# An LSTM layer with a residual: the last four, not eight, steps from plain products in two half banks each, a new column order, and a new order at the head

## The chip, the core and the metric

The kernel runs on one core of a Trainium2 chip. TensorE multiplies into PSUM (eight banks, 128 partitions of 512 fp32 each), ScalarE and VectorE do the element-wise work, GpSimd adds the residual, and SyncE (SP) issues the DMAs. The metric is the device time of one execution in microseconds (us), the median of three runs. A profiled execution of the same program gives the page and the trace that are quoted; it has its own time and, within that, its span from the first to the last recorded instruction.

## What is computed

```
x: (32, 512, 512)   h0: (32, 512)   Wx, Wh: (512, 2048)   b: (2048)
xW = x @ Wx + b                       # per step t: (32, 2048), gates i f o g
c  = 0;  h = h0
for t in 0..511:
    a = xW[:, t] + h @ Wh
    c = sigmoid(a_f) * c + sigmoid(a_i) * tanh(a_g)
    h = sigmoid(a_o) * tanh(c)
    out[:, t] = x[:, t] + h
```

All of it is in fp32. The steps are a chain: step t + 1 needs the h of step t.

## The kernel before

**Layout.** A step's pre-activations a fill one PSUM bank: partition j * 32 + b for the j-th block of 128 units and batch row b, and along the free axis four gates (G) of 128 units. A product with 512 columns is four matmul calls, one for each j, on four column groups of TensorE; each fp32 call shows as two MATMUL instructions in the trace. The banks are three accumulators pa, one pb, one pp, and the gate banks ge (even steps) and go[0], go[1] (odd steps), chosen by gates_of (L88).

**The input product.** Four consecutive steps are a quad. For quads FIRST = 2 to LAST - 1 = 125 (steps 8 to 503), x Wx of the four steps is made by a fast matrix product in two levels (Strassen's scheme in Winograd's form): 7 outer products r = 1 to 7, each of 7 inner products s = 1 to 7, that is 49 products of 128 columns in place of the 64 that plain products have. Operands are sums of blocks of x (early_sums L115, late_sums L132) and differences of blocks of Wx (outer_weight L196, inner_weight L200, scheduled by weights and make_weights). Results are collected by adds, copies and seeds in evacuate (L385), and end in the gate banks before h Wh is added there. Each r runs in its own windows (BEGIN), and input_part (L420) issues those of window k.

**Plain products.** Steps 0 to 7 and 504 to 511 have x Wx from direct (L345): for each of four pairs (k, gg), two blocks e and four j, 256 columns each. At the end these go to the banks in last_banks as the fast products release them; which pair goes into which window is set by the loop over todo (L551), by the room left beside the fast products. The bias enters by a copy into the bank ahead (set_bias) or an add behind (add_bias). reload (L209) brings back part of the raw Wx, which w_5 had overwritten.

**The order.** All instructions are put out in program order per engine (manual_schedule), with no reordering by a planner. The loop over windows k = 8 to 522 does, for step t = k - 11: h_part(t) (L448: h Wh, 16 calls of 512 columns), then evacuate, bias, sums and weights for VectorE and ScalarE, then input_part and direct as TensorE's filler, then cell(t) (L460). h_part(t + 1) waits for the transposed h of cell(t), so the filler is what TensorE does while the cell runs. In cell, sigmoid (i, f), tanh (g) and sigmoid (o) are three ScalarE instructions over all 128 units of a partition; products, sum, tanh of c, h and the transpose go in two halves of 64 units, so that h_part(t + 1) can begin with the first half (ht[:, 0:2]).

**The head.** SP issues, in this order, the bias row, chunk 0 of x (eight steps), raw Wx (0,0), chunk 1, raw (0,1), (1,0), (1,1), h0 and Wh in quarters. TensorE clears banks (clear, first_bias), then runs first_direct (L534), plain products of steps 2, 0, 1 and 3 while the raw weights arrive, and step 4's into pp.

**The end.** After step 511, x is added to the transposed halves of h in the tile last (L491), and one DMA stores it (L492).

Of the kernel before, what the change touches and what calls it, by code (L numbers as in the profile page):

```python
# [11 lines left out]
P = 128  # L12
B = 32
# [6 lines left out]
FIRST = 2  # L20
LAST = T // 4 - 2

LEAD = 11
BEGIN = {1: 0, 5: 1, 6: 3, 7: 6, 2: 7, 3: 7, 4: 9}
WINDOWS = T + LEAD


@with_exitstack
def kernel(
# [7 lines left out]
    out: bass.AP,  # L37
):


# [45 lines left out]

    last_banks = [pa[1], pa[0], pp, pb, pa[2], go[0], ge, go[1]]

    def gates_of(t):
        if t >= 4 * LAST:  # L90
            return last_banks[t - 4 * LAST]
        return ge if t % 2 == 0 else go[(t % 4) // 2]
# [85 lines left out]
    def load_raw(k, gg):  # L178
# [3 lines left out]
        )  # L182

    bias_row = w_sb[7][0:1, 0:NJ].rearrange("p s j u -> p s (j u)")
    nc.sync.dma_start(out=bias_row, in_=bias.rearrange("j g u -> j (g u)").unsqueeze(0))
    load_chunk(0)
    load_raw(0, 0)
    load_chunk(1)
    load_raw(0, 1)
    load_raw(1, 0)  # L190
    load_raw(1, 1)
    nc.sync.dma_start(out=h_init.rearrange("p q b -> p (q b)"), in_=h0)
    for k in range(NJ):
# [37 lines left out]

    def clear(bank):

        for j in range(NJ):
            nc.tensor.matmul(
                bank[j * B : (j + 1) * B],
                c_init[:, 0:B],
                c_init.unsqueeze(1).to_broadcast([P, 4, P]),
                start=True,
                stop=True,  # L240
            )

    def first_bias(bank):

        for j in range(NJ):
            nc.tensor.matmul(bank[j * B : (j + 1) * B], ones, bias_row[:, j], start=True, stop=True)
# [97 lines left out]

    def direct(t, pairs, bank=None):  # L345

        c, tt = divmod(t, TC)
        bank = gates_of(t) if bank is None else bank
        fresh = not written(bank)
        for k, gg in pairs:  # L350
            for e in range(2):
                for j in range(NJ):
                    nc.tensor.matmul(  # L353
                        bank[j * B : (j + 1) * B, 2 * gg : 2 * gg + 2],
                        xcs[c][:, tt, 2 * k + e],
                        raw_blocks(k, gg, e, t >= 4 * LAST)[:, :, j],
                        start=fresh and (k, gg, e) == (0, 0, 0),
                        stop=True,
                        skip_group_check=True,
                    )  # L360
# [86 lines left out]
    state = {"c": c_init, "ht": h_init}  # L447

    def h_part(t):
        g = gates_of(t)  # L450
        for k in range(NJ):
            for j in range(NJ):
                nc.tensor.matmul(  # L453
                    g[j * B : (j + 1) * B],
                    state["ht"][:, k, :],
                    wh_sb[:, k, j, :],
                    start=False,
                    stop=True,
                    skip_group_check=True,
                )  # L460

    def cell(t):
        n, tt = divmod(t, TC)
        g = gates_of(t)
        s = work.tile([P, G, P], F32, name=f"s_{t}", tag="s")
        nc.scalar.activation(s[:, 0:2, :], g[:, 0:2, :], AF.Sigmoid)  # L466
        nc.scalar.activation(s[:, 3, :], g[:, 3, :], AF.Tanh)
        nc.scalar.activation(s[:, 2, :], g[:, 2, :], AF.Sigmoid)
        fc = work.tile([P, P], F32, name=f"fc_{t}", tag="fc")
# [3 lines left out]
        ht = work.tile([P, NJ, B], F32, name=f"ht_{t}", tag="ht", bufs=3)  # L473
        halves = [slice(0, P // 2), slice(P // 2, P)]
        nc.vector.tensor_mul(fc, s[:, 1, :], state["c"])  # L475
        for u in halves:
            nc.vector.tensor_mul(ig[:, u], s[:, 0, u], s[:, 3, u])  # L477
        for u in halves:
            nc.vector.tensor_add(c[:, u], fc[:, u], ig[:, u])  # L479
        for u in halves:  # L480
            nc.scalar.activation(tc_t[:, u], c[:, u], AF.Tanh)  # L481
        for u in halves:
            nc.vector.tensor_mul(h[:, u], s[:, 2, u], tc_t[:, u])  # L483
        for i, u in enumerate(halves):
            nc.vector.transpose(ht[:, 2 * i : 2 * i + 2].rearrange("p q b -> p (q b)"), h[:, u])  # L485
        state["c"], state["ht"] = c, ht
        if t == T - 1:
            last = opool.tile([P, 2, NJ, B], F32, name="last", tag="oc")
            for i in range(2):
                q = slice(2 * i, 2 * i + 2)  # L490
                nc.vector.tensor_add(last[:, 0, q], xcs[n][:, tt, q], ht[:, q])  # L491
            nc.sync.dma_start(out=out[n][:, tt * P :], in_=last[:, 0].rearrange("p q b -> p (q b)"))  # L492
            return
        if tt % 2 == 0:
# [11 lines left out]
        0: [(5, 6)],  # L506
        1: [(1, 4), (5, 7), 6, (6, 5)],
        2: [(5, 4), (6, 6)],
        3: [(6, 7)],
# [19 lines left out]
    bias_at = {12: (2,), 13: (5,), 14: (4,), 15: (7,), 16: (6,)}  # L529
    direct_at = {k: [(t, ALL) for t in bias_at[k] if t not in (2, 4)] for k in bias_at}  # L530
    direct_at[11], direct_at[12] = [(3, ALL[2:3])], [(3, ALL[3:4])]

    def first_direct(k):

        pairs = {8: ALL[0:2], 9: ALL[2:3], 10: ALL[3:4]}.get(k, ())
        for pair in pairs:
            direct(2, (pair,), gates_of(3))
            if k == 10:
                park(2, gates_of(3), "u3")
                set_bias(3)  # L540
            for t in (0, 1):
                direct(t, (pair,))
        if k == 10:
            direct(3, ALL[0:2])

    end = 4 * LAST
    free_at = (504, 509, 510, 510, 512, 513, 514, 515)
    todo = [(end + i, (pair,)) for i in range(8) for pair in ALL]
    bias_after = {}
    for k in range(504, WINDOWS):  # L550
        bias_at[k] = tuple(end + i for i in range(8) if free_at[i] == k and written(gates_of(end + i)))  # L551
        count = sum(
            n
            for r in BEGIN
            for stage, n in enumerate((2, 1, 1, 2 if r == 2 else 3, 1 if r == 2 else 0))
            if quad_at(r, k, stage) is not None
        )
        room = (12 - count) // 4 if k < 513 else 2 + k % 2
        direct_at[k] = []
        while todo and free_at[todo[0][0] - end] <= k and room > 0:  # L560
            t = todo[0][0]
            direct_at[k].append(todo.pop(0))
            room -= 1
            if not written(gates_of(t)):
                bias_after[t] = k + 1
        assert not todo or todo[0][0] > k - LEAD + 1
    assert not todo

    with tc.manual_schedule():
        warm = work.tile([P, G, P], F32, name="warm", tag="s")  # L570
        nc.scalar.activation(warm[:, 0], c_init, AF.Sigmoid)
        nc.vector.memset(xr1, 0.0)
        for bank in (go[1], ge):
            clear(bank)
        first_bias(pp)
        clear(go[0])
        nc.vector.tensor_copy(go[1], pp)
        nc.scalar.copy(bias_sb, pp)
        for t in (0, 1):
            set_bias(t)  # L580
        make((1, 5))
        make((1, 6))
        start_sums()
        first = early_sums(nc.vector, 1)
        for op in first[:6]:
            op()
        make((1, 7))
        make(5)
        for op in first[6:]:
            op()  # L590
        make((5, 5))
        early, late = {}, {}
        for k in range(4 * FIRST, WINDOWS):
# [4 lines left out]
            if k == 4 * LAST + 1:  # L598
                reload()
            if t >= 0:  # L600
                h_part(t)
            evacuate(k)
            for i in bias_at.get(k, ()):
                set_bias(i)
            for i in bias_after:
                if bias_after[i] == k:
                    add_bias(i)
            for first, sums_of, made, cut in ((-1, early_sums, early, 5), (3, late_sums, late, 3)):
                c, rest = divmod(k - first, TC)
                if (2 if sums_of is early_sums else 1) <= c < NCHUNK - 1 and rest in (0, 2):  # L610
                    if rest == 0:
                        made[c] = sums_of(nc.vector, c)
                    for op in made[c][:cut] if rest == 0 else made.pop(c)[cut:]:
                        op()
            make_weights(k)
            if t < 0:
                first_direct(k)
            input_part(k)
            if k == 10:
# [11 lines left out]
def _laid_out(name, a):  # L631
# [7 lines left out]
    elif name == "L0_cond_Wx":  # L639

        a = a.reshape(NJ, 2, 2, B, 2, 2, NJ, P).transpose(1, 4, 0, 3, 2, 5, 6, 7).reshape(4, P, 4 * NJ * P)
    elif name == "L0_cond_Wh":
        a = a.reshape(NJ, NJ, B, G, NJ, P).transpose(0, 2, 1, 4, 3, 5).reshape(P, NJ, NJ, G * P)
    else:
        a = a.reshape(G, NJ, P).transpose(1, 0, 2)
    return _np.ascontiguousarray(a)
# [22 lines left out]
```

## Time and profile before

| | us |
|---|---|
| median of 3 runs | 3161.65 |
| lowest, highest run | 3161.55, 3162.08 |
| the profiled execution | 3161.6 |
| its span | 3159.8 |
| h Wh (L453), sum of its groups, busy | 1852.3 |
| VectorE, ScalarE, GpSimd busy | 2233.7, 1275.6, 237.1 |
| DMA, mean rate over the span | 27 GB/s |

The granted TensorE clock is 9 in each of the page's 40 slices (90% of full speed or more), and 1.0 as the mean of the run. In rows of the trace, the first number is the start in the span, the second the busy time, then engine, line, operation, output and input tile, shapes and count; a bracket gives the idle time ahead of it and what released it. Matmul rows overlap: one ends later than the next one starts, so distances of starts tell the pace.

### The profile page before, as it was taken

The page shows a single profiled execution, that of the slowest core. Times are in us where ns is not written, and L with a number is a line of the kernel's source. Part 1 is how long each engine was busy: PE and PEld are TensorE (multiplying, and loading weights), DVE is VectorE, ACT ScalarE, POOL GpSimd, SP SyncE. Part 2 cuts the span into 40 slices and gives each one's busy share as a digit, 9 for nine tenths or more (in the row PEclk, how much of TensorE's full clock was granted, in tenths as well). Part 3 has the DMA queues.
Part 4 walks back from the last instruction along what each step waited for, and adds up shares of the span by engine and source line. Part 5 has one row for each costly group of instructions (what it writes and reads, how often), then busy time and mean ns, then how long its engine had stood idle before and what let it go on. Part 6 is the DMA issues. An engine that isn't in the chain of part 4 may idle for free.

```text
span 3159.8 us, 149296 instructions
## 1 busy us (share of the span) xinstructions
PE 3148.7 (100%) x66048; PEld 1897.1 (60%) x66048; DVE 2233.7 (71%) x9239; ACT 1275.6 (40%) x4191; POOL 237.1 (8%) x515
## 2 busy tenths in 40 slices
PE   9999999999999999999999999999999999999999
PEld 5666666666666666666666666666666666666653
DVE  7777777777777777777777777777777777777763
ACT  2444444444444444444444434444444444443432
POOL 0000000000000000000000000000000000000000
PEclk9999999999999999999999999999999999999999
DMA  3000000000000000000000000000000000000010
GB/s 134 28 26 21 26 21 27 26 21 26 28 20 28 20 28 26 21 26 21 26 26 21 26 28 20 28 20 28 26 21 26 23 25 28 20 26 28 20 34 13
DMA packets 48460, 86.19 MB, mean 27 GB/s; under 512 B 5313, under 2 KB 38337, under 8 KB 46785
## 3 DMA queue, kind: packets, MB, share of 16 engines
q1 hardware_dynamic: 47810, 76.64, 7.3%
q8 instruction: 516, 8.45, 1.1%
q14 instruction: 134, 1.10, 0.1%
HBM read 43.07 MB, written 33.55 MB: 24 GB/s over the span
## 4 chain that ended last, share of the span: by engine, by line
PE 99%; DVE 1%; DMA 0%; ACT 0%; issue 0%; SPq 0%; DVEq 0%; ACTq 0%
PE ge L453 28%; PE go L453 27%; PE pa L325 18%; PE pp L325 10%; PE pb L325 6%; PE ge L325 5%; PE go L325 3%; PE go L353 1%; PE pa L453 0%; PE ge L353 0%; PE pa L353 0%; DMA w<-in_L_cond_Wx_dram 0%; PE pp L353 0%; PE pp L453 0%; PE pb L453 0%; ACT s L466 0%
## 5 line engine op out<-in xcount | busy, mean ns | idle before, releaser
L453 PE MATMUL go<-wh_sb,ht 128*32 128x512 f32 x8128 | 918.7, 592 | 0.1
L453 PE MATMUL ge<-wh_sb,ht 128*32 128x512 f32 x8064 | 911.5, 592 | 1.4 <-DVE ht L485 1.2
L475 DVE TENSOR_TENSOR fc<-s,c 128x128 f32<-128x128 f32 x511 | 149.6, 293 | 566.9 <-ACT s L466 566.9
L453 PEld LDWEIGHTS go<-wh_sb,ht 128*32 128x32 f32 x8128 | 256.7, 110 | 458.3 <-issue 454.5
L453 PEld LDWEIGHTS ge<-wh_sb,ht 128*32 128x32 f32 x8064 | 256.8, 110 | 456.3 <-issue 415.6
L496 POOL TENSOR_TENSOR oc<-xc,ht 128x128 f32<-128x128 f32 x511 | 236.9, 464 | 2913.9 <-DVE ht L485 1457.9
L466 ACT ACTIVATE s<-ge 128x256 f32<-128x256 f32 x253 | 97.1, 384 | 828.8 <-PE ge L453 828.8
L325 PE MATMUL pa<-w,n 128*32 128x128 f32 x5952 | 299.2, 273 | 0.0
L481 ACT ACTIVATE ig<-c 128x64 f32<-128x64 f32 x1024 | 205.9, 248 | 222.1 <-DVE c L479 222.1
L466 ACT ACTIVATE s<-go 128x256 f32<-128x256 f32 x254 | 97.5, 384 | 442.8 <-PE go L453 442.8
L483 DVE TENSOR_TENSOR fc<-s,ig 128x64 f32<-128x64 f32 x1024 | 190.2, 225 | 96.4 <-ACT ig L481 96.4
L325 PEld LDWEIGHTS pa<-w,n 128*32 128x32 f32 x5952 | 181.1, 110 | 76.7 <-issue 39.7
L325 PEld LDWEIGHTS pa<-w,na 128*32 128x32 f32 x3968 | 124.3, 110 | 148.5 <-issue 110.5
L265 ACT COPY u<-pp 128x512 f32<-128x512 f32 x248 | 145.2, 585 | 141.9 <-PE pp L325 141.9
L325 PE MATMUL pa<-w,na 128*32 128x128 f32 x3968 | 200.0, 273 | 0.0
L325 PE MATMUL pp<-w,sa 128*32 128x128 f32 x3968 | 199.4, 273 | 0.0
L325 PE MATMUL pa<-w,nb 128*32 128x128 f32 x3968 | 199.4, 273 | 0.0
L485 DVE STREAM_TRANSPOSE ht<-fc 128x64 f32<-128x64 f32 x1024 | 190.5, 224 | 1.7 <-DVE fc L483 1.3
L477 DVE TENSOR_TENSOR ig<-s 128x64 f32<-128x64 f32 x1024 | 181.1, 218 | 0.0
L479 DVE TENSOR_TENSOR c<-fc,ig 128x64 f32<-128x64 f32 x1024 | 181.0, 218 | 0.0
L395 DVE TENSOR_TENSOR p<-u,p 128x512 f32<-128x512 f32 x124 | 86.0, 694 | 114.5 <-ACT u L265 114.5
L325 PEld LDWEIGHTS pa<-w,nb 128*32 128x32 f32 x3968 | 121.4, 110 | 74.1 <-issue 37.6
(139 smaller groups left out, 5289.2 us busy)
## 6 DMA issues: line engine op xcount, KB each, us to landing
xc<-in_x_dram SPq DMA_DIRECT2D x64, 512.0 KB, 3.9
out_dram<-oc SPq DMA_DIRECT2D x255, 128.0 KB, 1.7
w<-in_L_cond_Wx_dram SPq DMA_DIRECT2D x4, 1024.0 KB, 9.4
wh_sb<-in_L_cond_Wh_dram SPq DMA_DIRECT2D x4, 1024.0 KB, 17.9
w<-in_L_cond_Wx_dram SPq DMA_DIRECT2D x2, 512.0 KB, 6.3
h_init<-in_cond_dram SPq DMA_DIRECT2D x1, 64.0 KB, 13.5
out_dram<-oc SPq DMA_DIRECT2D x1, 64.0 KB, 1.6
out_dram<-last SPq DMA_DIRECT2D x1, 64.0 KB, 1.6
```

The costliest lines, as they stand in the source:

```text
L265: nc.scalar.copy(u, pp)
L325: nc.tensor.matmul(dst[j * B : (j + 1) * B], operand(r, s, quad), w_sb[r][:, place(r, s), j], start=start, stop=True, skip_group_check=True,)
L395: nc.vector.tensor_add(U["p5", q], U[4, q], U["p5", q])
L453: nc.tensor.matmul(g[j * B : (j + 1) * B], state["ht"][:, k, :], wh_sb[:, k, j, :], start=False, stop=True, skip_group_check=True,)
L466: nc.scalar.activation(s[:, 0:2, :], g[:, 0:2, :], AF.Sigmoid)
L475: nc.vector.tensor_mul(fc, s[:, 1, :], state["c"])
L477: nc.vector.tensor_mul(ig[:, u], s[:, 0, u], s[:, 3, u])
L479: nc.vector.tensor_add(c[:, u], fc[:, u], ig[:, u])
L481: nc.scalar.activation(tc_t[:, u], c[:, u], AF.Tanh)
L483: nc.vector.tensor_mul(h[:, u], s[:, 2, u], tc_t[:, u])
L485: nc.vector.transpose(ht[:, 2 * i : 2 * i + 2].rearrange("p q b -> p (q b)"), h[:, u])
L496: nc.gpsimd.tensor_add(state["oc"][:, tt % 2], xcs[n][:, tt], ht)
```

## The change

It does the following.

- LAST goes from 126 to 127: steps 504 to 507 become quad 126 of the fast product, and steps 508 to 511 alone are plain.
- Each of these four has two banks (last_banks is now four pairs), one for each half of the units: half_of(t, h). h_part issues h Wh for them by halves, in the order A01, B01, A23, B23 (the number is the block of h), and for step 511 A0123, B0123. cell handles half A in full, then half B.
- The columns of Wx, Wh and the bias are in the order half, gate, unit (host layout _laid_out), so that a half's four gates are together; in every cell, a gate is then two runs of 64 in the bank and in s.
- In step 511, x is added to h before any transpose (x_last is transposed in the window of step 498), each half is stored by a DMA of its own, and the host undoes the other layout.
- At the head, the bias row goes through ScalarE's DMA queue, chunk 0 is loaded in two halves (the second behind the raw weights), first_direct takes steps 1, 0, 2 and 3 with three banks cleared and the bias spread into ge, adds the bias of step 1 afterwards, and does all four steps' first two pairs together. Two pairs of step 5 move one window ahead. The weight differences of r = 6 move one window back.
- The last plain products stand in a table by window (last_at).

```diff
-LAST = T // 4 - 2
+LAST = T // 4 - 1
...
-    last_banks = [pa[1], pa[0], pp, pb, pa[2], go[0], ge, go[1]]
+    last_banks = [(pa[1], pa[0]), (pp, pb), (pa[2], go[0]), (ge, go[1])]
+
+    def half_of(t, h):
+
+        return last_banks[t - 4 * LAST][h][:, 0:2]
...
+    def load_steps(i):
+
+        if 0 not in xcs:
+            xcs[0] = xpool.tile([P, TC, NJ, B], F32, name="xc_0", tag="xc")
+        nc.sync.dma_start(
+            out=xcs[0][:, 4 * i : 4 * i + 4].rearrange("p t q b -> p (t q b)"),
+            in_=x[0][:, 4 * i * P : 4 * (i + 1) * P],
+        )
...
-    nc.sync.dma_start(out=bias_row, in_=bias.rearrange("j g u -> j (g u)").unsqueeze(0))
-    load_chunk(0)
+    nc.scalar.dma_start(out=bias_row, in_=bias.rearrange("j g u -> j (g u)").unsqueeze(0))
+    load_steps(0)
     load_raw(0, 0)
     load_chunk(1)
     load_raw(0, 1)
     load_raw(1, 0)
     load_raw(1, 1)
+    load_steps(1)
...
     def h_part(t):
-        g = gates_of(t)
-        for k in range(NJ):
+
+        if t < 4 * LAST:
+            order = [(gates_of(t).rearrange("p n u -> p (n u)"), slice(0, G * P), k) for k in range(NJ)]
+        else:
+            halves = [(half_of(t, i).rearrange("p n u -> p (n u)"), slice(i * G * H, (i + 1) * G * H)) for i in range(2)]
+            if t < T - 1:
+                order = [(*z, k) for kk in (0, 2) for z in halves for k in (kk, kk + 1)]
+            else:
+                order = [(*z, k) for z in halves for k in range(NJ)]
+        for g, u, k in order:
...
+    def x_last():
+
+        state["x"] = work.tile([P, P], F32, name="x_last")
+        nc.vector.transpose(state["x"], xcs[NCHUNK - 1][:, TC - 1].rearrange("p q b -> p (q b)"))
...
+        for part in ([(0, 1)] if t < 4 * LAST else [(0,), (1,)]):
+            g = by_gate(gates_of(t) if t < 4 * LAST else half_of(t, part[0]))
...
+            nc.scalar.activation(s[:, n2, 0:2], g[:, :, 0:2], AF.Sigmoid)
+            nc.scalar.activation(s[:, n2, 3], g[:, :, 3], AF.Tanh)
+            nc.scalar.activation(s[:, n2, 2], g[:, :, 2], AF.Sigmoid)
+            nc.vector.tensor_mul(both(fc), s[:, n2, 1], both(state["c"]))
...
+            if t == T - 1:
+                nc.vector.tensor_add(tc_t[:, units], h[:, units], state["x"][:, units])
+                nc.sync.dma_start(out=out[n][:, tt * P + units.start : tt * P + units.stop], in_=tc_t[:, units])
+                continue
...
-        1: [(1, 4), (5, 7), 6, (6, 5)],
-        2: [(5, 4), (6, 6)],
+        1: [(1, 4), (5, 7)],
+        2: [6, (6, 5), (5, 4), (6, 6)],
...
+        13: [(5, ALL[0:2])],
+        14: [(5, ALL[2:4])],
...
+        banks = {1: go[0], 0: ge, 2: go[1], 3: pp}
+        if k == 8:
+            for pair in ALL[0:2]:
+                for t in banks:
+                    direct(t, (pair,), banks[t], t == 1)
+        elif k == 9:
+            for t in (2, 0, 1):
+                direct(t, ALL[2:3], banks[t])
+        elif k == 10:
+            for t in (2, 0, 1):
+                direct(t, ALL[3:4], banks[t])
+            park(2, go[1], "u3")
+            nc.scalar.copy(go[1], pp)
+            nc.scalar.copy(pp, bias_sb)
+            add_bias(1)
...
+    free_at = ((508, 513), (514, 514), (516, 517), (518, 519))
+    last_at = {
+        509: [(0, 0, 0)],
+        511: [(0, 0, 1)],
+        513: [(0, 1, 0)],
+        514: [(0, 1, 1)],
+        515: [(1, 0, 0), (1, 0, 1)],
+        516: [(1, 1, 0), (1, 1, 1)],
+        517: [(2, 0, 0), (2, 0, 1)],
+        518: [(2, 1, 0), (2, 1, 1)],
+        519: [(3, 0, 0), (3, 0, 1)],
+        520: [(3, 1, 0)],
+        521: [(3, 1, 1)],
+    }
...
             if k == 4 * LAST + 1:
                 reload()
+                x_last()
...
+            for i, h in bias_before.get(k, ()):
+                nc.scalar.copy(half_of(i, h), bias_sb[:, 2 * h : 2 * h + 2])
+            for i, h in bias_after.get(k, ()):
+                nc.vector.tensor_add(half_of(i, h), half_of(i, h), bias_sb[:, 2 * h : 2 * h + 2])
```

## The prediction

> **What bounds the kernel now.** I read the page first: engine shares, then the chain of waits.
>
> ```profile
> PE 3148.7 (100%) x66048; PEld 1897.1 (60%) x66048; DVE 2233.7 (71%) x9239; ACT 1275.6 (40%) x4191; POOL 237.1 (8%) x515
> PE 99%; DVE 1%; DMA 0%; ACT 0%; issue 0%; SPq 0%; DVEq 0%; ACTq 0%
> ```
>
> TensorE is the bound almost everywhere, so the first question is how many columns it streams. A busy PE hides short stalls, though, because a matmul's row lasts longer than its issue slot. So I next took the PE timeline and read starts, not durations:
>
> ```profile
> 1003.99 3.62 PE L453 MATMUL go<-wh_sb,ht 128*32 128x512 f32 x32
> 1007.43 0.40 PE L325 MATMUL pa<-w,n 128*32 128x128 f32 x8
> 1007.64 0.40 PE L325 MATMUL pa<-w,na 128*32 128x128 f32 x8
> ...
> 1010.26 3.62 PE L453 MATMUL ge<-wh_sb,ht 128*32 128x512 f32 x32
> ...
> 1016.54 3.62 PE L453 MATMUL go<-wh_sb,ht 128*32 128x512 f32 x32
> ...
> 1022.59 3.62 PE L453 MATMUL ge<-wh_sb,ht 128*32 128x512 f32 x32
> ```
>
> h Wh takes 3.43 us from its start to the next row; an input product of 128 columns (8 instructions; I call it a **unit**) takes 0.2185. A steady step is 3.43 + 0.2185 f with f = 13, 13, 12, 11 units: 6.27, 6.27, 6.05, 5.83 us. A pair of a plain product (16 instructions of 256 columns) takes 0.86 to 0.87, four units.
>
> The third view is the same timeline at the end, where steps are short of filler:
>
> ```profile
> 3132.81 3.64 PE L453 MATMUL pa<-wh_sb,ht 128*32 128x512 f32 x32 [0.47 <-DVE ht L485]
> 3138.86 3.62 PE L453 MATMUL go<-wh_sb,ht 128*32 128x512 f32 x32
> 3144.70 3.64 PE L453 MATMUL ge<-wh_sb,ht 128*32 128x512 f32 x32 [0.50 <-DVE ht L485]
> 3150.75 3.62 PE L453 MATMUL go<-wh_sb,ht 128*32 128x512 f32 x32
> ```
>
> Plain steps alternate 8 and 12 units. The 8-unit step should take 3.43 + 1.75 = 5.18 but takes 5.84: PE waits for the transposed h. The cell's chain needs 2.33 to 2.41 us after h Wh's last issue, so no step is shorter than 5.76 to 5.84 (I take **5.80**). The 11-unit step (5.83) hides the cell by only 0.07.
>
> **Part 1: four steps move from plain to fast products.** 64 units become 49. From the instruction orders, all filler falls from 6253 to 6238 units; the 95 ahead of step 0 stay. If PE were the bound everywhere: 15 x 0.2185 = 3.28 us less. At the end it isn't, so I add the steps up. Start at step 493 (3044.73): before, 3159.8 - 3044.73 = 115.07. After, steps 493 to 507 have 12, 11, 13, 13, 10, 12, 11, 11, 6, 11, 10, 10, 11, 8, 8 units: two at 6.27, two at 6.05, five at 5.83, six at 5.80 = 88.59. The added quad's sums, evacuations and copies are those of every steady quad, whose 11-unit steps hide them. The reload of the weights moves four windows on: on SP it waits for the last product with r = 5 (step 497), lands 6.3 us later and is read in step 500, over 15 us on; the stores of out behind it keep nobody waiting, as GpSimd's adds alternate between two tiles 11 us apart. x_last's transpose and the halves' bias adds (about 0.3 and 0.41) sit on VectorE at the start of windows, under 3.43 us of h Wh.
>
> **Part 2: halves in steps 508 to 511.** Two sets of 256 columns cost TensorE the same (L353's 16 rows of 256 take 0.863, 54 ns each, against 107 for 512 columns): 3.45 instead of 3.43. What they win is the cell. h Wh(A) ends 0.86 us before h Wh(B). The chain of half A, from rows: last issue to sigmoid 0.25; sigmoid and tanh 0.16 apart, tanh 0.25, 0.04 to the product: product at +0.45; sum at +0.70; tanh of c at +0.95 (64 columns: 0.248); h at +1.24; transpose at +1.50, end +1.72, PE at +1.80. So PE may start the next step 2.05 after A's last issue, which is 2.59 into the step: a floor of 4.64 instead of 5.80. Half B is queued behind A on ScalarE (A's tanh of c, at +1.20 after A's last issue) and on VectorE (A's transpose): B's transpose is ready 3.42 after A's last issue. The order A01 B01 A23 B23 asks for it at 2.05 + 1.73 = 3.78, so it hides.
> - 508 (8 units): 3.45 + 1.73 = 5.18, PE-bound; 509 and 510 (4 units, 4.32): floor 4.64 each.
> - 511 takes A0123 first and needs half B at 2.05 + 0.86 = 2.91, before 3.42: PE waits 0.51; B ends 3.96 into the step.
>
> **Part 3: the last output.**
>
> ```profile
> 3154.43 0.38 ACT L466 ACTIVATE s<-go 128x256 f32<-128x256 f32 x1 [4.41 <-PE go L453]
> ...
> 3156.28 0.37 DVE L485 STREAM_TRANSPOSE ht<-fc 128x64 f32<-128x64 f32 x2
> 3156.81 0.36 DVE L491 TENSOR_TENSOR last<-xc,ht 128x64 f32<-128x64 f32 x2 [0.16 <-DVE ht L485]
> 3157.20 0.33 SPq L492 DMA_DIRECT2D out_dram<-last  x1
> ```
>
> h's transposes go from the end; x_last's transpose sits in an early step. Sigmoid to store: 1.75 (h at +1.24, add +1.50, end +1.72) instead of 2.77; store to the end of the span 2.60 as now. Step 511 to the end: 3.96 + 0.25 + 1.75 + 2.60 = 8.56 (before 9.05). Here a rule speaks against the change: the Trainium skill, DMA: Bandwidth & Descriptors, Specifications, says transfers under 512 B are read, changed and written back, and the halves of the store have rows of 256 B. The rows: 128 KB land in 1.7, 64 KB in 1.6 us, so size hardly counts; no row has 256 B. By the row 0; if the rule doubled the landing, +1.6. I take 0, the nearest row, and keep +1.6 for the range.
>
> Tail: 88.59 + 5.18 + 2 x 4.64 + 8.56 = 111.61, **3.46 less**.
>
> **Part 4: the head.**
>
> ```profile
> 10.94 1.07 PE L353 MATMUL go<-w,xc 128*32 128x256 f32 x16 [0.90 <-DMA w<-in_L_cond_Wx_dram]
> 25.68 0.60 PE L453 MATMUL ge<-wh_sb,h_init 128*32 128x512 f32 x3
> 45.37 3.65 PE L453 MATMUL go<-wh_sb,ht 128*32 128x512 f32 x32
> 51.29 3.64 PE L453 MATMUL ge<-wh_sb,ht 128*32 128x512 f32 x32 [0.75 <-DVE ht L485]
> 8.38 0.33 SPq L194 DMA_DIRECT2D wh_sb<-in_L_cond_Wh_dram  x1
> wh_sb<-in_L_cond_Wh_dram SPq DMA_DIRECT2D x1, 1024.0 KB, 19.1
> ```
>
> The bias leaves SP's queue (one issue, 0.42 us) and half of chunk 0 (256 KB; 0.64 us at the 410 GB/s that the windows show) goes behind the raw weights. So these land 1.06 earlier (7.06, 10.9, 13.4, 17.4 become 6.0, 9.8, 12.3, 16.3). ScalarE's queue, where it goes, has nothing before the copies at about 5.5 to delay. PE then starts at 6.15, has 16 units for each of the first two weights instead of 12, waits 0.3 once, and reaches step 0 at 23.55, not 25.69. But Wh's last quarter lands at 8.38 + 19.1 = 27.5. All bytes ahead of it are the same, so it moves by 0.42 alone, to 27.1, and step 0 wants it 2.57 in, at 26.1. PE stalls for 1.0, and step 0 ends 1.1 (by issues) to 1.4 (by its last matmul) earlier: **1.38 less**. Step 2 loses 8 units (7.76 to 6.05 by PE), but VectorE has the same list there, 6.80 from transpose to transpose (37.23 to 44.03): 6.72, 1.04 less. Step 3 gains 8 units: 3.43 + 15 x 0.2185 = 6.71 instead of 5.92, 0.79 more. The bias of step 1 becomes an add on VectorE that waits for that step's last raw product (19.65); behind it queue the weight differences of r = 6 (2.29 + 3 x 0.69, to about 24.7), two seeds and sums (to 27.4). The first product with r = 6 and the cell of step 0 come after 27.9, so this hides; had it no cover, each us late there is a us on step 0. ScalarE's park and two copies (3 x 0.6 from 18.1) are done at 19.9, as PE asks for pp at 20.1. Head: 1.38 + 1.04 - 0.79 = **1.63 less**.
>
> **Part 5: the new column order**, in all 512 cells: gates become runs of 64 instead of 128. Rows: ScalarE's L316 (two runs) 597 ns against 584 to 592 for whole copies; VectorE's L127 (runs of 64) 418 against L251's 416. So +0 to +13 ns, inside the 0.07 of the 11-unit steps: 0. Without that cover, each 10 ns costs 1.24 us over 124 such steps; a gain is excluded, since PE bounds these.
>
> **Sum.** The profiled execution took 3161.6 (span 3159.8 and 1.8 around it), 0.05 under the median of 3161.65. 3161.6 - 3.46 - 1.63 = **3156.5**, 0.16% less.
>
> **Rivals.**
> - **Wh doesn't bind step 0** (0.25). For it: the DMA engines' mean share falls to 0.53 at 26 to 27 us, so most of Wh was there sooner. Against it: the landing of 19.1. Step 0 then ends 2.14 earlier: 3155.8; if VectorE doesn't bind step 2 either, 3155.1.
> - **The halves don't overlap** (0.12): B's pieces hold A's up on the in-order engines, as the strict order of parts allows if A's tanh of c is late. Steps 508 to 510 stay at 5.80, the end at 9.05: 115.04, tail gain 0.03: 3159.9. Against it: ScalarE is only 40% busy.
> - **Slower** (0.06): the strided gates stretch every cell. It decides from +0.07 us a cell; +0.17 costs 124 x 0.10 = 12.4 in the 11-unit steps alone: 3168.9. The two-run rows speak against it.
> - The forecast's own case: 0.57, 3155.9 to 3157.4.
>
> **From these the numbers.** The range runs from the first rival's far end, 3155.0, up past the forecast plus the store's 1.6, to 3158.6. A difference under 0.2% (6.3 us) counts as no change, about what a measurement can tell. Under 3155.3 lies half of the first rival and a little of the forecast: faster 0.16; slower 0.06; same 0.78.
>
> **What would show it.** In the profile after: steps of 5.18 and twice 4.64 at 508 to 510 with A's transpose as releaser; a PE wait for a DMA of Wh in step 0 at about 27; step 2 at 6.7 released by VectorE; 11-unit steps still 5.83. Wrong if those grow, if step 0 has no wait, or if ScalarE's sigmoid of half B starts much later than 1.35 after A's.

## The result, and the profile after

| | before | after |
|---|---|---|
| median, us | 3161.69 (22 runs) | 3156.68 (22 runs) |
| lowest, highest run | 3160.99, 3163.21 | 3156.42, 3159.3 |
| profiled execution (span) | 3161.6 (3159.8) | 3156.65 (3154.9) |

The ratio is 0.9985, with a 95% interval of 0.9979 to 0.9991: 5.0 us less, 0.18 from the predicted 3156.5 and inside its range. By the prediction's bound of 0.2% this counts as no change; the interval leaves 1 out, so the kernel is faster, by 0.15%.

The page of the changed kernel reads as the one before: TensorE bounds almost everything. Its busy times and its chain of waits:

```profile
PE 3146.2 (100%) x66312; PEld 1898.6 (60%) x66312; DVE 2247.4 (71%) x9289; ACT 1282.4 (41%) x4217; POOL 237.1 (8%) x515
PE 99%; DVE 1%; ACT 0%; issue 0%; ACTq 0%; DVEq 0%
```

TensorE's busy time falls by 2.5 us and VectorE's grows by 13.7, off the chain. The rest is read from the timeline, by starts. Head, a steady stretch, and end of the changed kernel (start, duration, engine, line, operation; the bracket is idle time and its releaser):

```profile
6.33 1.20 PE L263 MATMUL ge<-w,ones 1*32 1x512 f32 x8
7.45 1.07 PE L373 MATMUL go<-w,xc 128*32 128x256 f32 x16
...
24.58 3.62 PE L485 MATMUL ge<-wh_sb,h_init 128*32 128x512 f32 x32
...
30.28 3.64 PE L485 MATMUL go<-wh_sb,ht 128*32 128x512 f32 x32
...
36.17 3.64 PE L485 MATMUL ge<-wh_sb,ht 128*32 128x512 f32 x32
...
42.88 3.64 PE L485 MATMUL go<-wh_sb,ht 128*32 128x512 f32 x32 [0.47 <-DVE ht L530]
...
49.59 3.62 PE L485 MATMUL ge<-wh_sb,ht 128*32 128x512 f32 x32
...
2975.80 3.62 PE L485 MATMUL ge<-wh_sb,ht 128*32 128x512 f32 x32
2981.63 3.62 PE L485 MATMUL go<-wh_sb,ht 128*32 128x512 f32 x32
...
3131.70 3.66 PE L485 MATMUL pa<-wh_sb,ht 128*32 128x256 f32 x64 [0.47 <-DVE ht L530]
...
3136.91 1.05 PE L485 MATMUL pp<-wh_sb,ht 128*32 128x256 f32 x16
...
3141.72 1.07 PE L485 MATMUL pa<-wh_sb,ht 128*32 128x256 f32 x16 [0.31 <-DVE ht L530]
...
3144.33 1.05 PE L485 MATMUL go<-wh_sb,ht 128*32 128x256 f32 x16
3144.58 0.28 ACT L513 ACTIVATE s<-pa 128x128 f32<-128x128 f32 x1 [2.13 <-PE pa L485]
...
3145.29 0.23 DVE L520 TENSOR_TENSOR c<-fc,ig 128x64 f32<-128x64 f32 x1
3145.61 0.26 ACT L522 ACTIVATE ig<-c 128x64 f32<-128x64 f32 x1 [0.52 <-DVE c L520]
3145.77 0.26 ACT L513 ACTIVATE s<-go 128x128 f32<-128x128 f32 x1
3145.90 0.23 DVE L524 TENSOR_TENSOR fc<-s,ig 128x64 f32<-128x64 f32 x1 [0.38 <-ACT ig L522]
...
3146.26 0.25 DVE L530 STREAM_TRANSPOSE ht<-fc 128x64 f32<-128x64 f32 x1
...
3146.55 1.07 PE L485 MATMUL ge<-wh_sb,ht 128*32 128x256 f32 x16 [0.31 <-DVE ht L530]
...
3147.32 0.22 DVE L524 TENSOR_TENSOR fc<-s,ig 128x64 f32<-128x64 f32 x1 [0.32 <-ACT ig L522]
3147.58 0.24 DVE L530 STREAM_TRANSPOSE ht<-fc 128x64 f32<-128x64 f32 x1
3147.88 1.07 PE L485 MATMUL ge<-wh_sb,ht 128*32 128x256 f32 x16 [0.25 <-DVE ht L530]
...
3150.74 0.28 ACT L513 ACTIVATE s<-go 128x128 f32<-128x128 f32 x1 [0.45 <-PE go L485]
...
3152.26 0.22 DVE L526 TENSOR_TENSOR ig<-fc,x_last 128x64 f32<-128x64 f32 x1
```

- **Head.** Step 4 starts at 49.59 (before 51.29): 1.70 earlier. Step 0 starts at 24.58 (before 25.68), step 3 is released by VectorE at 42.88, 6.71 after step 2. The prediction had named a step 0 without a wait for Wh as a sign of being wrong, and there is none: its h Wh is one unbroken row of 3.62, and step 1 follows 5.70 later.
- **Steady steps.** The 11-unit step is still 5.83 (2975.80 to 2981.63), so what the head won stands: step 493 starts at 3043.04, 1.69 earlier.
- **End.** Steps 493 to 507 take 88.66. Steps 508, 509 and 510 take 5.21, 4.81 and 4.83 (3131.70, 3136.91, 3141.72, 3146.55), and 511 to the end of the span 8.35. Together 111.86 (before 115.07): 3.21 less.

### The profile page after: what moved, and what is told of

Same layout as the page of the kernel before. It is cut to its first block, busy times and chain, and to the rows that moved or that the text cites. A ratio compares the mean times of both kernels' runs of the same rounds, so it can differ in the third digit from the quotient of the medians.

```text
span 3154.9 us, 149903 instructions
## 1 busy us (share of the span) xinstructions
PE 3146.2 (100%) x66312; PEld 1898.6 (60%) x66312; DVE 2247.4 (71%) x9289; ACT 1282.4 (41%) x4217; POOL 237.1 (8%) x515
## 4 chain that ended last, share of the span: by engine, by line
PE 99%; DVE 1%; ACT 0%; issue 0%; ACTq 0%; DVEq 0%
PE ge L485 28%; PE go L485 28%; PE pa L342 18%; PE pp L342 10%; PE pb L342 6%; PE ge L342 5%; PE go L342 3%; PE go L373 0%; PE ge L373 0%; PE pp L373 0%; PE pa L485 0%; DVE w L215 0%; PE go L252 0%; PE pa L373 0%; ACT ig L522 0%; DVE fc L524 0%
## 5 line engine op out<-in xcount | busy, mean ns | idle before, releaser
L516 DVE TENSOR_TENSOR fc<-s,c 128x128 f32<-128x128 f32 (+1 forms) x515 | 149.9, 291 | 545.0 <-ACT s L513 545.0
L522 ACT ACTIVATE ig<-c 128x64 f32<-128x64 f32 x1024 | 206.3, 248 | 224.6 <-DVE c L520 224.6
L513 ACT ACTIVATE s<-go 128x256 f32<-128x256 f32 (+1 forms) x256 | 98.4, 384 | 436.8 <-PE go L485 436.8
L530 DVE STREAM_TRANSPOSE ht<-fc 128x64 f32<-128x64 f32 x1022 | 190.5, 224 | 2.3 <-DVE fc L524 1.3
```

Source lines behind the costliest of these rows:

```text
L513: nc.scalar.activation(s[:, n2, 0:2], g[:, :, 0:2], AF.Sigmoid)
L516: nc.vector.tensor_mul(both(fc), s[:, n2, 1], both(state["c"]))
L522: nc.scalar.activation(tc_t[:, HALVES[i]], c[:, HALVES[i]], AF.Tanh)
```

## Experiments

Each kernel is the changed kernel with the edit shown; the diffs are cut to their core. The kernel before ran beside them at 3161.57 to 3161.7.

### Head and end are separate gains

With the head of before (its DMA order, its first plain products, its windows for the weights), the rest as changed:

```diff
-    nc.scalar.dma_start(out=bias_row, in_=bias.rearrange("j g u -> j (g u)").unsqueeze(0))
-    load_steps(0)
+    nc.sync.dma_start(out=bias_row, in_=bias.rearrange("j g u -> j (g u)").unsqueeze(0))
+    load_chunk(0)
...
-    load_steps(1)
...
-        for bank in (go[1], pp, go[0]):
+        for bank in (go[1], ge):
```

> The changed kernel with the head of the kernel before (bias and whole chunk 0 on SP, old first products, old windows for the weights). Theory (head and tail are separate gains; the head's is 1.70 us by step 4's start, 51.29 to 49.59): about 3158.4 us, step 4 starts at 51.3, steps 493 to 511 as in the changed kernel. Rival (the new column order or the added quad costs something that the head pays back): more than 3159; rival (the head gains nothing that lasts): 3156.7.

Measured: 3158.32 (3158.02 to 3159.71), ratio 0.9990 (0.9981 to 0.9999). The end alone gives 3161.7 - 3158.32 = 3.4, the head 3158.32 - 3156.68 = 1.64. In its trace step 4 starts at 51.17, and steps 493 to 511 take 111.9, as in the changed kernel. Its first raw product takes 1.51 from start to start, the second 0.86, which matters below:

```profile
8.19 1.68 PE L372 MATMUL go<-w,xc 128*32 128x256 f32 x16
9.70 1.04 PE L372 MATMUL ge<-w,xc 128*32 128x256 f32 x16
```

### The halves alone

The last four steps from plain products, but with one bank each and the whole cell:

```diff
-    last_banks = [(pa[1], pa[0]), (pp, pb), (pa[2], go[0]), (ge, go[1])]
+    last_banks = [(b, b) for b in (pa[1], pp, pa[2], ge)]
...
-        for part in ([(0, 1)] if t < 4 * LAST else [(0,), (1,)]):
+        for part in [(0, 1)]:
```

> The changed kernel with the last four steps as whole products in one bank each (pa[1], pp, pa[2], ge) and the whole cell of the other steps; same filler by windows, same last add. Theory (the halves turn a floor of 5.8 into one of 4.8): steps 508 to 510 take 5.80 to 5.84 each instead of 5.21, 4.81, 4.83, that is 2.6 us more, step 511 to the end about 8.4; 3159.3 us. Rival (the halves' extra instructions eat their gain): 3156.7 to 3157.5.

Measured: 3159.66 (3159.28 to 3159.96), ratio 0.9994 (0.9985 to 1.0003). PE timeline, steps 509 to 511:

```profile
3137.61 3.64 PE L480 MATMUL pp<-wh_sb,ht 128*32 128x512 f32 x32 [0.47 <-DVE ht L525]
3143.44 3.64 PE L480 MATMUL pa<-wh_sb,ht 128*32 128x512 f32 x32 [1.33 <-DVE ht L525]
3149.31 3.64 PE L480 MATMUL ge<-wh_sb,ht 128*32 128x512 f32 x32 [1.36 <-DVE ht L525]
```

The steps stay at 5.83 and 5.87, however little filler they have, and TensorE idles up to 1.36. The halves are worth 3159.66 - 3156.68 = 3.0. Of the 2.0 that this kernel keeps, the head is 1.64, so the four plain steps fewer save about 0.4 by themselves.

### Filler where it is free

Step 508 is bound by TensorE (8 units), 509 by the cell. Two of 508's units go into step 507, where TensorE waited for the transpose:

```diff
+    bias_before.setdefault(518, []).append(bias_before[519].pop())
+    direct_at[518].append((end + 3, ((0, 0),), None, False, (0,)))
+    direct_at[519][0] = (end + 3, ((0, 0),), None, False, (1,))
```

> The changed kernel with one block (2 units) of the plain product for step 511 moved from step 508's filler to step 507's: fillers 10, 6, 4, 4 in place of 8, 8, 4, 4. Theory (507 has room under the whole cell's 5.84, 508 is bound by TensorE at 5.21 and would fall to the halves' floor of 4.82): 0.39 less, 3156.3 us; 507 stays at 5.84. Rival (508's step is not bound by its filler): 3156.7.

Measured: 3156.48 (3156.16 to 3157.26), ratio 0.9984 (0.9975 to 0.9992), the lowest median of the kernels that compute the whole. Head and end in its PE timeline:

```profile
4.46 1.51 PE L252 MATMUL go<-c_init 128*32 128x512 f32 x8
5.91 1.06 PE L263 MATMUL ge<-w,ones 1*32 1x512 f32 x8
6.90 1.07 PE L373 MATMUL go<-w,xc 128*32 128x256 f32 x16
...
27.46 1.07 PE L485 MATMUL ge<-wh_sb,h_init 128*32 128x512 f32 x8 [0.60 <-DMA wh_sb<-in_L_cond_Wh_dram]
...
3132.04 3.66 PE L485 MATMUL pa<-wh_sb,ht 128*32 128x256 f32 x64
3136.85 1.07 PE L485 MATMUL pp<-wh_sb,ht 128*32 128x256 f32 x16
```

Step 508 takes 4.81, not 5.21: the gain of 0.40 is there in the trace. The medians show only 0.2 of the 0.39 expected, the lowest runs 0.26. In this execution step 1 started at 30.62, not 30.28, and everything up to the end is 0.34 late. The head is the same code as the changed kernel's, and behaves otherwise: it waits for Wh. That opened the question of what sets the head, below.

### Two more edits at the end

Beside the last edit, step 511 in the order A01 B01 A23 B23, and half B's first sigmoid ahead of half A's tanh of c:

```diff
-            if t < T - 1:
-                order = [(*z, k) for kk in (0, 2) for z in halves for k in (kk, kk + 1)]
-            else:
-                order = [(*z, k) for z in halves for k in range(NJ)]
+            order = [(*z, k) for kk in (0, 2) for z in halves for k in (kk, kk + 1)]
...
+            if part == (0,):
+                nc.scalar.activation(s[:, 1:2, 0:2], by_gate(half_of(t, 1))[:, :, 0:2], AF.Sigmoid)
```

> As the rebalanced one, and step 511 takes h Wh in the order of the other three (A01 B01 A23 B23), and half B's first sigmoid goes ahead of half A's tanh of c on ScalarE. Theory (the wait in step 511 is for half B's h, and B's cell is queued behind A's on ScalarE): no PE wait inside step 511, step 511 to the end 8.0 instead of 8.35, so 3155.9 us. Rival (A's tanh of c is pushed out by B's sigmoid and the floor of 508 to 510 grows by about 0.15 each): 3156.3 or more.

Measured: 3156.68 (3156.39 to 3156.84), ratio 0.9984 (0.9975 to 0.9993): 0.2 more than with the first edit alone, and not the 3155.9 expected. The number lies where the rival put it, but not for its reason: steps 509 and 510 take 4.84 each, so the early sigmoid costs the next step nearly nothing. Step 511's wait is gone and half B's sigmoid comes 3.73 after the step's start (3146.43), instead of 4.19. Yet the end stays:

```profile
3150.16 0.28 ACT L520 ACTIVATE s<-go 128x128 f32<-128x128 f32 x1 [0.35 <-PE go L482]
...
3150.87 0.23 DVE L526 TENSOR_TENSOR ig<-fc,x_last 128x64 f32<-128x64 f32 x1
3151.01 0.22 DVE L514 TENSOR_TENSOR fc<-s,c 128x64 f32<-128x64 f32 x1
...
3152.20 0.23 DVE L526 TENSOR_TENSOR ig<-fc,x_last 128x64 f32<-128x64 f32 x1
```

Half B's first product on VectorE (3151.01) stands in program order behind half A's last add (3150.87), and A is now later, since B's matmuls stand between its own. The end of TensorE's wait became a wait on VectorE: the last add comes 5.77 after the step's start, against 5.71 in the changed kernel.

### What each delay in the cell costs

Sigmoid of o ahead of tanh of g in every cell:

```diff
-            nc.scalar.activation(s[:, n2, 3], g[:, :, 3], AF.Tanh)
             nc.scalar.activation(s[:, n2, 2], g[:, :, 2], AF.Sigmoid)
+            nc.scalar.activation(s[:, n2, 3], g[:, :, 3], AF.Tanh)
```

> The changed kernel with sigmoid(o) put ahead of tanh(g) in every cell, so that the product i*g comes about 0.12 us later (tanh ends 0.75 after the first sigmoid's start, the product starts now at 0.63). It measures what a longer cell costs. Theory (11-unit steps hide 0.07 us, 12-unit steps 0.29): 125 x 0.05 = 6 us more, 3162.7 us, 11-unit steps 5.88, 12- and 13-unit steps unchanged. Rival (no cover at all): 125 x 0.12 = 15, 3171.7. Rival (more cover than I read): 3156.7 to 3157.5.

Measured: 3168.37 (3168.08 to 3168.79), ratio 1.0022 (1.0013 to 1.0030): 11.7 more than the changed kernel. A steady cell in its timeline:

```profile
1003.67 0.38 ACT L513 ACTIVATE s<-ge 128x256 f32<-128x256 f32 x1 [3.04 <-PE ge L485]
...
1004.10 0.28 ACT L515 ACTIVATE s<-ge 128x128 f32<-128x128 f32 x1
...
1004.42 0.36 DVE L518 TENSOR_TENSOR ig<-s 128x64 f32<-128x64 f32 x2
```

The product comes 0.75 after the sigmoid, instead of 0.63: 0.12, as expected. The 11-unit step grows by 0.06 (to 5.89), so the other 0.06 of the delay is covered by its filler. A TensorE that has waited loses a little more at its restart: the first filler comes 3.46, not 3.43, after the start of such a step's h Wh (136 steps of this trace; ten in the changed kernel's). So a quad of four steps takes 24.51, not 24.43. Step 493 starts 10.1 later (3053.14 against 3043.04; 0.6 of it is there at step 1 already), and from it to the end it is 1.6 more (113.46 against 111.86). The 6 us expected left the restart and the end's cell-bound steps out; the 15 us of the rival left the cover out.

### What sets the head

First the bias DMA back on SP's queue, ahead of chunk 0, the rest as changed; then that, with the last quarter of step 0's h Wh taken from Wh's third quarter, so that it doesn't wait for Wh's last DMA (this leaves that quarter's product out in step 0):

```diff
-    nc.scalar.dma_start(out=bias_row, in_=bias.rearrange("j g u -> j (g u)").unsqueeze(0))
+    nc.sync.dma_start(out=bias_row, in_=bias.rearrange("j g u -> j (g u)").unsqueeze(0))
...
-                    wh_sb[:, k, j, u],
+                    wh_sb[:, 2 if t == 0 and k == 3 else k, j, u],
```

> The changed kernel with the bias row's DMA back at the front of SP's queue, nothing else. Theory (the late bias holds TensorE, but Wh's last quarter would hold step 0 just behind it): raw products start at about 6.8 instead of 7.45, step 0 starts at about 24.2 instead of 24.58, then waits for Wh, which comes 0.42 later (27.3); step 0 ends 0.1 to 0.4 later than in the changed kernel; 3156.8 to 3157.1 us. Rival (the start of TensorE sets the head): step 0 ends 0.4 to 0.65 earlier, 3156.0 to 3156.3.

> As the one with the bias on SP, and step 0's last quarter of h Wh is multiplied by Wh's third quarter (so the true last quarter's product is left out in step 0 alone, and with it the wait for that DMA; all else is computed from there). Theory (Wh's last quarter binds once TensorE starts earlier): step 0 has no wait and ends 0.4 to 0.7 earlier than with the bias on SP alone, about 0.3 earlier than in the changed kernel: 3156.3 us. Rival (Wh never binds): the same as with the bias on SP alone, within 0.1.

Measured: 3157.03 (3156.72 to 3159.33) and 3156.39 (3156.06 to 3159.86). In the first one's trace, step 0's last quarter starts at 27.47 after a wait for Wh; without that DMA 0.64 goes. So with the bias on SP, Wh's landing binds step 0. The head of the changed kernel, with its late raw products (7.45 instead of 6.15) and no wait, then looked like another case, in which a bias that lands late by ScalarE's queue holds TensorE up. Three more runs tested that: the changed kernel again; the same with step 0's last quarter left out as above, but the bias on ScalarE's queue; and with one more clear ahead of the bias.

```diff
-        for bank in (go[1], pp, go[0]):
+        for bank in (go[1], pp, go[1], go[0]):
```

> The changed kernel once more, unaltered, for a second trace of the same head. In the traces so far the raw products begin at 6.53 to 7.67 us, always after the bias matmuls without a recorded wait, because TensorE's first matmuls take 214 ns each and later ones 107 to 110, and the turn comes at another time in each execution (before the third clear ends in some, after the bias in others). Theory (the turn of TensorE's pace sets the head, and Wh lands just behind): 3156.7 within 0.2; step 1 anywhere from 30.1 to 30.9; a wait for Wh in step 0 if the raw products begin before about 7.2, none if later. Rival (the bias lands late by ScalarE's queue, always): the raw products begin at 7.45 again, with a recorded wait for that DMA or the same gap, step 1 at 30.28.

> The changed kernel, with step 0's fourth quarter of h Wh taken from the third quarter of Wh: that part of the product is left out in step 0 alone, so that nothing waits for Wh's last landing. Theory (TensorE's own start and Wh's landing are within half a us of each other, and which ends last differs between executions): 0.1 to 0.4 less than the changed kernel, 3156.3 to 3156.6. Rival 1 (Wh's landing binds step 0 by 1.0, as predicted): at least 0.6 less, 3156.1 or under. Rival 2 (Wh never binds with the bias on ScalarE's queue): 3156.7, no difference.

> The changed kernel with one more clear of a bank ahead of the bias: TensorE's raw products begin 0.86 later if that clear runs at the later pace, 1.71 if at the first. Theory (TensorE asks for Wh's last quarter at 26.7 to 27.2, and it lands at 27.1 to 27.6): TensorE now asks at 27.6 to 28.5, nothing waits for Wh, and the end comes 0.4 to 1.2 later: 3157.1 to 3157.9. Rival (as predicted, TensorE is 1.0 ahead of Wh at step 0): 0 to 0.5 later, 3156.7 to 3157.2, with the wait for Wh still in step 0.

Measured: 3156.62 (3156.43 to 3157.01), 3156.27 (3155.64 to 3156.77) and 3156.68 (3156.32 to 3157.76). The PE timeline of the second, without Wh's last quarter:

```profile
2.76 1.51 PE L252 MATMUL pp<-c_init 128*32 128x512 f32 x8
4.10 1.03 PE L252 MATMUL go<-c_init 128*32 128x512 f32 x8
5.06 1.06 PE L263 MATMUL ge<-w,ones 1*32 1x512 f32 x8
6.30 1.07 PE L373 MATMUL go<-w,xc 128*32 128x256 f32 x16 [0.17 <-DMA w<-in_L_cond_Wx_dram]
...
23.59 3.62 PE L485 MATMUL ge<-wh_sb,h_init 128*32 128x512 f32 x32
```

And of the third, from its third clear on (the row of 16 is the third and the fourth clear):

```profile
4.46 2.96 PE L252 MATMUL go<-c_init 128*32 128x512 f32 x16
7.35 1.06 PE L263 MATMUL ge<-w,ones 1*32 1x512 f32 x8
8.34 1.07 PE L373 MATMUL go<-w,xc 128*32 128x256 f32 x16
25.47 3.62 PE L485 MATMUL ge<-wh_sb,h_init 128*32 128x512 f32 x32
```

Where each trace's head stands (us; "full pace" is where the first entry of the trace's clock record begins, "asks" is step 0's start plus the 2.58 to its last quarter, landings are the trace's own records):

| run | full pace from | raw products | asks for Wh's last quarter | it lands | step 1 |
|---|---|---|---|---|---|
| without Wh's last quarter (e_q2) | 3.72 | 6.30 | does not wait (26.17) | 26.93 | 29.29 |
| whole cells at the end (e_whole) | 4.54 | 6.53 | 26.44 | 27.16 | 30.35 |
| swapped cell (e_swap) | 4.71 | 6.63 | 26.92 | 27.57 | 30.90 |
| moved filler (e_rebal) | 5.42 | 6.90 | 26.69 | 27.42 | 30.62 |
| changed kernel again (e_again) | 5.97 | 7.17 | 26.88 | 27.12 | 30.31 |
| changed kernel | 6.66 | 7.45 | 27.15 | 26.84 | 30.28 |
| two edits at the end (e_tail) | 7.10 | 7.67 | 27.38 | 26.76 | 30.50 |
| fourth clear (e_clear4) | 6.61 | 8.34 | 28.05 | 27.98 | 31.17 |

- **The bias isn't late.** No trace has a bracket at L263, and its row follows the clears within 0.16 of their pace: at 5.06 without Wh's last quarter and 5.91 in the trace of the moved filler, both by ScalarE's queue. The head of before, with the bias on SP, has the same 0.16 (e_old_head). That theory falls.
- **TensorE's pace differs between executions.** A clear takes 1.71 at first (1.05 to 2.76 in the rows of before, shown with part 4 below: 214 ns for each of 8 instructions of 512 columns) and 0.96 in the trace without Wh's last quarter from 4.10 to 5.06. The pace turns within the second clear in the trace without Wh's last quarter, within the third in that of the moved filler, within the fourth in that of the fourth clear, and in the bias matmuls after 6.33 in the changed kernel's. So the raw products of this head start between 6.30 and 7.67, by the execution. The views print a granted clock of 1.00 throughout; the clock record behind them has no entry before the turn, and its first one begins where the rows turn fast. The Trainium skill, TensorE: Matmul & The Clock Gate, Part 1, describes half rate until an activity window of 3.4 us, which runs freely, has been busy. Eleven of the twelve turns lie between 3.72 and 7.10, one such window apart. The twelfth does not fit: with the head of before (e_old_head) TensorE kept half pace until 9.47, and why stays open.
- **Wh's landing differs too.** Its last quarter landed between 26.76 and 27.57 in the six traces with this head and this wait. In four of them TensorE asked first and waited for it; in the changed kernel's and in that of the two edits it had landed before. Step 1 starts by whichever comes last. Of the 0.34 that the moved filler's trace was late, TensorE's start has no part (it was 0.47 earlier); the landing was 0.58 later. What moves the landing was not tried.
- **Wh cuts off the early side.** Without Wh's last quarter the runs spread over 1.1 us, down to 3155.64; with it they start at 3156.42.
- **In the median execution Wh binds, by about 0.35** (3156.62 - 3156.27, 11 runs each, with ranges that overlap).
- **The extra clear changes the median by nothing**, though its four highest runs lie 0.3 to 1.1 above it. My expectation of 0.4 to 1.2 missed; the rival's number was right, but the wait that it named is not in the trace. The profiled execution (3157.61) was not late by the clear: Wh landed at 27.98 there, 0.07 before TensorE asked. A wait of 0.35 does not cover a clear of about 0.9, so what absorbed it in the median execution is not shown.
- **The bias on SP** costs about what its issue takes: the lowest runs are 3156.72 against 3156.42 and 3156.43, the medians 0.35 to 0.41 apart, for an issue of 0.41. (The kernel before read 3161.70 beside it and 3161.57 beside the second of those, so 0.28 to 0.35.) The traces alone could not say so: step 1 starts at 30.62 in one with it and in one without.

## Why the prediction was right, by its steps

- **Part 1, four steps to fast products: right.** Steps 493 to 507 took 88.66, summed as 88.59.
- **Part 2, halves: mechanism right, size 0.39 short.** 508 took 5.21 (5.18), 509 and 510 4.81 and 4.83 (4.64 each). The mis-sized term is the floor of "2.05 after A's last issue": it is 2.22, from 3144.33, where half B's last block follows A's, to 3146.55. The rows give the place. Sigmoid to product and to sum are as summed (0.45 and 0.71). Then half A's tanh of c starts 0.32 after the sum, where 0.25 was taken, and the transpose 0.36 after h (3145.90 to 3146.26), where 0.26 was. Half B, in the same step, needs just 0.25 and 0.26 (the latter from 3147.32 to 3147.58). The views of these two lines of the kernel (L522 and L530, for 3145 to 3149) show what stands in A's gaps: an EVENT_SEMAPHORE in ScalarE's queue (17 ns, at 3145.5) ahead of A's tanh and one in VectorE's (50 ns, at 3146.2) ahead of A's transpose, and none ahead of B's. Two comparisons in the same trace point the same way: in step 511 half A's h is followed by an add without such an instruction, after 0.26; and the first transposes of steps 0 to 2, which have none, come 0.29 after h, those of step 3 and later whole cells, which have one, 0.33 (48.08 to 48.42). No run removed them.
- **Step 511: right.** TensorE waits for B's transpose, released at 3147.88, about 0.47 later than the 0.86 of A's blocks would let it (0.51 summed), and B ends 3.94 into the step (3.96).
- **Part 3, the end: right, 0.21 too high.** From the last sigmoid (3150.74) to the last add 1.52, as summed (1.50), and from there to the end 2.64, where 0.22 for the add and 2.60 for the store were taken. Halves of 32 KB with rows of 256 B landed in 1.5 us, against 1.6 for 64 KB with rows of 512 B. The rule of the Trainium skill, DMA: Bandwidth & Descriptors, Specifications, on transfers under 512 B does not show here; the nearest row was the better guide, and the 1.6 kept for the rule was not needed. These stores are half as large too, so no run separates the row's length from the size.
- **Tail: 3.21 less, predicted 3.46** (+0.07, +0.03, +0.36 and -0.21, by the four items above).
- **Part 4, the head: 1.70 by the traces, 1.64 by the runs, predicted 1.63.** The number is right, the path in parts, and in the changed kernel's own trace by luck. Step 2 (6.71, released by VectorE) and step 3 (6.71) are as summed. What it had wrong is the start: "PE then starts at 6.15 and reaches step 0 at 23.55", with "PE stalls for 1.0" after it. That holds for an execution with an early turn (6.30 and 23.59; Wh landed 0.8 after TensorE came to that place). But I took that as the one case. The turn of TensorE's pace was in the rows of before, which I read without asking what they meant: the first of these clears takes 1.71 (start to start), the bias row at 4.42 takes 0.99.

```profile
1.05 1.94 PE L235 MATMUL go<-c_init 128*32 128x512 f32 x8 [1.05 <-DVE ones L226]
2.76 1.73 PE L235 MATMUL ge<-c_init 128*32 128x512 f32 x8
4.42 1.06 PE L246 MATMUL pp<-w,ones 1*32 1x512 f32 x8
5.41 1.07 PE L235 MATMUL go<-c_init 128*32 128x512 f32 x8
```

In the changed kernel's trace step 0 started 1.03 later than summed (24.58), TensorE asked for Wh at 27.15, not 26.1, Wh had landed at 26.84, and the stall of 1.0 was nothing: one error took back the other. Step 0 is 1.10 earlier there and step 1 1.45, the predicted 1.1 to 1.4 with no wait in it. In the four traces that do wait, Wh's landing sets step 1, as the prediction had it (27.12 to 27.57, for 27.1).
- **Part 5, the column order: right.** Sigmoids of 384 and 385 ns, 11-unit steps of 5.83.
- **The rivals.** "The halves don't overlap" predicted 3159.9: that is what a kernel without halves takes (3159.66). "Wh doesn't bind step 0" was half right: in two of the six traces it does not, and 3155.64 is what it would give with an early turn (3155.8 predicted). The slower one has its mechanism confirmed by the swapped cell: past a cover of 0.06, a delay of 0.12 a cell costs 11.7; the new column order itself costs nothing of that.

## What to carry to other kernels

In a chain of steps, splitting the element-wise part by halves with a bank each takes its second half off the path only while the next product can begin with the first; the floor is then one half's chain, and every gap between dependent instructions in it counts fully, so take those gaps from rows of the same place in the chain. Where two bounds of the head lie within a microsecond of each other, one trace shows only which won that time: write down for each trace when one asks and when the other lands, then take one of them away and compare the spread and the lowest of many runs. After a wait on one engine is removed by a new order, look at what stands in program order on the next engine: in step 511 the gain of 0.46 at the sigmoid was gone two instructions later.

## What the runs showed that was not expected

TensorE's first matmuls ran at half their later pace (1.71 against about 0.9 us for 8 instructions of 512 columns), for 2.7 to 6.1 us after its first instruction in eleven traces and for 8.4 in the twelfth, while the views print a granted clock of 1.00. With a half-pace head of 8.4, step 4 still started at 51.17 (51.29 with a turn at 4.15), so TensorE's pace did not set the head of before in that trace. The same 1 MB of Wh landed up to 0.8 us apart between executions. After a step whose h Wh had waited for its operand, TensorE started the filler 0.03 late. An instruction with one semaphore instruction (EVENT_SEMAPHORE) ahead of it in its queue started 0.04 to 0.10 later than a like one without. Two stores of 32 KB in rows of 256 B landed no later than one of 64 KB in rows of 512 B.
